# Sigmoid and one silu from tanh, and one logarithm for both image halves, in a four-layer convolution and Mamba kernel

## The chip, the cores and the metric

The kernel runs on one core of a Trainium2 chip, as one program. The metric is the device time of one execution in microseconds (us); the median of several executions is given. All data are float32.

## The reference

The input x has 8 images of 384 channels and 32 x 32 pixels. Four layers follow one another. The change lies in the first two, so only these are shown in detail.

```python
# layer 0
x_norm = x * rsqrt(mean_over_channels(x * x) + 1e-6) * norm_w
# mamba, run once forward and once over the flipped sequence of the 1024 pixels
u, z = split(x_flat @ in_proj_w.T)            # 384 channels each
u = silu(causal_conv1d(u) + conv1d_b)
dt, Bm, Cm = split(u @ x_proj_w.T)
delta = softplus(dt @ dt_proj_w.T + dt_proj_b)
h = exp(delta * A) * h + delta * u * Bm        # 16 states per channel, pixel after pixel
y = (sum_over_states(h * Cm) + u * D) * silu(z)
global_feat = (fwd + bwd) @ out_proj_w.T * scale_mod
local_feat = sigmoid(conv3x3_depthwise(x_norm) + dw_b) * x_norm
x = x + res_scale * (global_feat + local_feat)
# layer 1
h = conv1x1(bn2(conv3x3_depthwise(conv1x1(bn1(x))))); x1 = h + x
qp, kp = phi(q), phi(k)                        # phi(t) = exp(t - t*t/2), 8 heads of 48
zz = 1 / (qp . sum_over_pixels(kp) + 1e-6)     # one per head and pixel
x2 = x1 + proj((qp @ (kp^T v)) * zz)
xn = (x2 - mean) * rsqrt(var + 1e-5)           # over channels
x = x2 + gelu(xn @ mlp_w1 + b1) @ mlp_w2 + b2
# layers 2 and 3: large depthwise convolutions, a 1x1 convolution, an exact gelu
```

## The kernel before, in words

The 384 channels are three tiles of 128 partitions (NC = 3), and an image of 1024 pixels is two halves of 512 (HALF)[...]. Layers 0 and 1 are in one function, `_layers01`; layers 2 and 3 follow for all images at once and are not touched.

Three generators produce the work of one image.

`front(b)` (line 572) is layer 0 up to the scan. For each half it squares x on ACT (ScalarE), takes the mean over the channels and its inverse root in `rsqrt_mean`, and scales x on DVE (VectorE). Then it projects x to u and z (lines 596 to 604): the u half is copied out of PSUM, the z half goes through Silu, and both are stored in HBM from ACT's DMA queue. Then the 3 x 3 convolution of the local branch runs on PE (TensorE), ACT takes its Sigmoid (line 615), and DVE multiplies by x_norm and adds to x (lines 618 and 619). Last come the u convolution with its Silu (line 645) and the softplus, which is made of Abs, Relu, Exp and Ln (lines 671 to 678).

`scan(b)` (line 695) is the recurrence. It has 48 passes (2 directions, 2 halves, 3 channel tiles, 4 groups of 4 states), each of two units. A unit takes two Exps on ACT (tile `da`, line 776), one product on DVE (`du`, line 781), two scan instructions on DVE (`hs`, line 793), one product on POOL (GpSimd, line 802), and PE then sums over the states into `acc` (line 736). There are four `da` buffers and eight `hs` buffers.

`layer1(b)` (line 877) is the second layer of one image: out projection, 1 x 1 convolution, 3 x 3 convolution, 1 x 1 convolution, keys and values pixel block by pixel block (phi is a Square and an Exp, lines 874 and 875), queries, the denominator `den` (line 1010) with its reciprocal `rz` made as exp(-ln(den)) (lines 1014 and 1015), its spreading over the channels by a matmul (`rzb`, line 1021), the projection, the layer norm (lines 1034 to 1051, again with `rsqrt_mean`) and the MLP with its Gelu (line 1062).

The loop at the end of `_layers01` goes over the images. While image b is scanned, `front(b + 1)` and `layer1(b - 1)` are advanced between the passes of the scan, each in proportion to the cost that it yields. `defer(n, fn)` puts work off until n + 1 passes have gone by. Within what this order gives as priority, a scheduler places the instructions of each engine and hands out the buffers; each engine then runs its instructions strictly in order. Short-lived tiles come from one tag, `t2`, of eleven buffers of 128 x 512.

An ACT function belongs to a table that has to be loaded first. The instruction ACT_TABLE_LOAD is placed by the compiler wherever the next function is not in the loaded table.

Of the kernel before, what the change touches and what calls it, by code (L numbers as in the profile page):

```python
# [8 lines left out]
FP = mybir.dt.float32  # L9
AF = mybir.ActivationFunctionType  # L10
ALU = mybir.AluOpType
# [3 lines left out]
P = 128  # L15
C = 384
NC = C // P
# [3 lines left out]
HALF = 512  # L21
# [353 lines left out]
def _layers01(tc, nc, B, xv, x2_d, dram, ident, mean_w, eps5, eps6, one, half, minus1, vec, bns, bnt,  # L375
# [12 lines left out]
    with ExitStack() as ctx:  # L388
        wp = ctx.enter_context(tc.tile_pool(name="w0", bufs=1))
# [23 lines left out]
        x1v, zv, udv, yfv = chunks(x1_d), chunks(z_d), chunks(ud_d), chunks(yf_d)  # L413
# [5 lines left out]
        def const(ap, shape, tag):  # L419
            t = wp.tile(shape, FP, tag=tag, name=tag)  # L420
            nc.scalar.dma_start(t, ap)
            return t

        wx = const(xproj_t.rearrange("(k p) e -> p k e", p=P), [P, NC, 64], "wx")
        wdt = wp.tile([P, C], FP, tag="wdt", name="wdt")
# [3 lines left out]
        spread = wp.tile([P, 4, P], FP, tag="spread", name="spread")  # L429
# [2 lines left out]
            nc.gpsimd.memset(spread[32 * j : 32 * j + 1, j, :], 1.0)  # L432
        t1 = const(taps1, [P, 2 * NG, 32], "t1")
        selt = const(sel, [P, 32], "selt")
        neg_a = const(alog, [P, NG, NR], "neg_a")
        nc.scalar.activation(neg_a, neg_a, AF.Exp)
        nc.vector.tensor_scalar_mul(neg_a, neg_a, -1.0)
        mask = const(headmask, [PR, PR], "mask")
        m8 = const(mask8.rearrange("(k p) e -> p k e", p=P), [P, NC, 32], "m8")
        nc.scalar.dma_start(wdt[32:64, :], mask8_t)  # L440


        zero = wp.tile([P, C + NC + 1], FP, tag="zero", name="zero")
# [12 lines left out]
        def psum(name):  # L456
            return psp.tile([P, HALF], FP, tag="mm", name=name, bufs=2)

        def long_psum(name):
            return psp.tile([P, HALF], FP, tag="mo", name=name)  # L460

        def t2(name):
            return sp.tile([P, HALF], FP, tag="t2", name=name, bufs=N_T2)
# [19 lines left out]
        def defer(n, fn):  # L483
            e = [n, fn]
            late.append(e)
            return e
# [29 lines left out]
        def rows(t):  # L516
            return t.rearrange("p (h w) -> p h w", w=W)
# [29 lines left out]
            )  # L547
            return ps

        def rsqrt_mean(srcs, eps, name):  # L550

            stat = psum(f"{name}_s")
            for k, src in enumerate(srcs):
                for j in range(4):
                    nc.tensor.matmul(
                        stat[32 * j : 32 * j + 32, 0:P], mean_w[:, 0:32], src[:, j * P : (j + 1) * P],
                        start=(k == 0), stop=(k == NC - 1), skip_group_check=True,
                    )
            r = t2(f"{name}_r")[:, 0:P]
            nc.scalar.activation(r, stat[:, 0:P], AF.Ln, bias=eps)  # L560
            nc.scalar.activation(r, r, AF.Exp, scale=-0.5)
            ps = psum(f"{name}_b")
            for j in range(4):
                nc.tensor.matmul(
                    ps[:, j * P : (j + 1) * P], spread[:, j, :], r, start=True, stop=True,
                    skip_group_check=True,
                )
            return ps

        def front(b):

            xn = []
            for h in range(2):
                cols = bass.ts(h, HALF)
                xh = a6(f"xi_{b}_{h}")
                nc.sync.dma_start(xh, xv[b][:, :, cols])
                sqs = [t2(f"sq_{b}_{c}_{h}") for c in range(NC)]
                for c in range(NC):  # L580
                    nc.scalar.activation(sqs[c], xh[:, c, :], AF.Square)
                rstd = rsqrt_mean(sqs, eps6, f"ms_{b}_{h}")
                t, mid = image6(f"xn_{b}_{h}")
                for c in range(NC):
                    nc.vector.scalar_tensor_tensor(
                        mid[c], rows(xh[:, c, :]), vec("norm_w", c), rows(rstd), ALU.mult, ALU.mult
                    )
                put_image(xn_d, b % 2, h, t, nc.gpsimd)
                xn.append(mid)
                yield 3  # L590
            uo = u_d[b % 2].rearrange("(c p) i -> p c i", p=P)
            for e in range(2):
                w = wtile(inproj_t[:, e * C : (e + 1) * C], f"win_{b}_{e}")
                for h in range(2):
                    for m in range(NC):
                        ps = psum(f"in_{b}_{e}_{m}_{h}")
                        dense(ps, w, m, xn[h])
                        t = t2(f"uz_{b}_{e}_{h}_{m}")
                        if e == 0:
                            nc.scalar.copy(t, ps)  # L600
                            nc.scalar.dma_start(uo[:, m, 3 + h * HALF : 3 + (h + 1) * HALF], t)
                        else:
                            nc.scalar.activation(t, ps, AF.Silu)
                            nc.scalar.dma_start(zv[b][:, m, bass.ts(h, HALF)], t)
                        yield 3


# [1 line left out]
            for h in range(2):  # L609
                for c in range(NC):  # L610
                    xr = t2(f"xr_{b}_{h}_{c}")
                    nc.sync.dma_start(xr, xv[b][:, c, bass.ts(h, HALF)])
                    ps = conv3(xn_d, b % 2, h, c, t3, f"lc_{b}_{h}_{c}")
                    lc = t2(f"lg_{b}_{c}_{h}")
                    nc.scalar.activation(lc, ps, AF.Sigmoid, bias=vec("dw_b0", c))

                    def local(h=h, c=c, lc=lc, xr=xr):
                        nc.vector.tensor_mul(rows(lc), rows(lc), xn[h][c])
                        nc.vector.scalar_tensor_tensor(xr, lc, rs, xr, ALU.mult, ALU.add)
                        nc.gpsimd.dma_start(x1v[b][:, c, bass.ts(h, HALF)], xr)  # L620

                    defer(1, local)
                    yield 3


            for h in range(2):
                cols = bass.ts(h, HALF)
                ucs = [a6(f"uc_{b}_{h}_{d}") for d in range(2)]
                for c in range(NC):
                    uts = []  # L630
                    for j in range(4):
                        ut = sp.tile([P, 18 * (W + 2)], FP, tag="im", name=f"ut_{b}_{h}_{c}_{j}", bufs=N_IM)
                        src = bass.AP(
                            u_d.tensor, u_d[b % 2, 32 * (4 * c + j), h * HALF].offset,
                            [[UL, 32], [1, 4], [1, HALF + 3]],
                        )
                        nc.sync.dma_start(ut[:, 0 : HALF + 3], src)
                        uts.append(ut)
                    for d in range(2):
                        ps = psum(f"c1_{b}_{h}_{c}_{d}")  # L640
# [8 lines left out]
                ps = psum(f"xd_{b}_{h}")  # L649
                for k in range(NC):  # L650
                    for d in range(2):
                        nc.tensor.matmul(
                            ps[64 * d : 64 * d + 64, :], wx[:, k, :], ucs[d][:, k, :],
                            start=(k == 0), stop=(k == NC - 1), skip_group_check=True,
# [7 lines left out]
                for c in range(NC):  # L662
                    dls, ts = [], []
                    for d in range(2):
                        ps = psum(f"dt_{b}_{h}_{d}_{c}")
                        at = slice(64 * d, 64 * d + DTR)
# [3 lines left out]
                        t, dl = t2(f"sp_{b}_{h}_{d}_{c}"), t2(f"dl_{b}_{h}_{d}_{c}")  # L670
# [206 lines left out]
        def layer1(b):  # L877
# [34 lines left out]
            for h in range(2):  # L912
# [19 lines left out]
                skip_group_check=True,  # L932
# [62 lines left out]
            yield 4  # L995


            qps, rzs, xns = [], [], []
            for h in range(2):
                qp = a6(f"qp_{b}_{h}")  # L1000
                qps.append(qp)
                for m in range(NC):
# [1 line left out]
                    dense(ps, wq, m, xx[h])  # L1004
                    phi(qp[:, m, :], ps, f"q_{b}_{h}_{m}")
                    yield 3
            for h in range(2):
                den = long_psum(f"den_{b}_{h}")
                for k in range(NC):
                    nc.tensor.matmul(  # L1010
                        den[32:64, :], ksv[:, k, :], qps[h][:, k, :], start=(k == 0), stop=(k == NC - 1)
                    )
                rz = t2(f"rz_{b}_{h}")
                nc.scalar.activation(rz[32:64, :], den[32:64, :], AF.Ln, bias=eps6[32:64])
                nc.scalar.activation(rz[32:64, :], rz[32:64, :], AF.Exp, scale=-1.0)
                rzs.append(rz)
                yield 3
            for h in range(2):
                for k in range(NC):
                    ps = long_psum(f"rzb_{b}_{h}_{k}")  # L1020
                    nc.tensor.matmul(
                        ps, wdt[32:64, k * P : (k + 1) * P], rzs[h][32:64, :], start=True, stop=True
                    )
                    nc.vector.tensor_mul(qps[h][:, k, :], qps[h][:, k, :], ps)
                yield 3
            for h in range(2):
                for m in range(NC):
                    ps = long_psum(f"pj_{b}_{h}_{m}")
# [5 lines left out]
            for h in range(2):  # L1034
                mu = long_psum(f"mu_{b}_{h}")
                for k in range(NC):
                    nc.tensor.matmul(mu, mean_w, xx[h][:, k, :], start=(k == 0), stop=(k == NC - 1))
                xn = a6(f"ln_{b}_{h}")
                xns.append(xn)
                for k in range(NC):  # L1040
                    nc.vector.tensor_sub(xn[:, k, :], xx[h][:, k, :], mu)
                yield 3
            for h in range(2):
                xn = xns[h]
                sqs = [t2(f"vs_{b}_{h}_{k}") for k in range(NC)]
                for k in range(NC):
                    nc.scalar.activation(sqs[k], xn[:, k, :], AF.Square)
                rstd = rsqrt_mean(sqs, eps5, f"var_{b}_{h}")
                for k in range(NC):
                    nc.vector.tensor_mul(xn[:, k, :], xn[:, k, :], rstd)  # L1050
                yield 3

            for h in range(2):
                acc = [long_psum(f"mo_{b}_{h}_{m}") for m in range(NC)]
# [159 lines left out]
```

## Time and profile before

| | |
|---|---|
| time before, median of 3 | 5797.18 us (5793.76 to 5818.33) |
| span of the profiled run | 5805.1 us |
| PE busy | 4813.5 us, 83% |
| DVE busy | 3677.1 us, 63% |
| ACT busy | 3064.5 us, 53% |
| POOL busy | 2892.9 us, 50% |
| mean granted TensorE clock | 0.896 |

A row of an instruction group reads: line, engine, operation, tile written and tiles read, shapes, count, then busy us and the mean ns of one, then the idle time of the engine just before these instructions and what ended most of it. PE busy time is modelled, since matmuls overlap, so a PE that is 90% busy need not be at its peak. PE's weight loads (PEld) run beside its matmuls. A float32 matmul shows as two records.

### The profile page before, as it was taken

The page shows a single profiled execution, that of the slowest core. Times are in us where ns is not written, and L with a number is a line of the kernel's source. Part 1 is how long each engine was busy: PE and PEld are TensorE (multiplying, and loading weights), DVE is VectorE, ACT ScalarE, POOL GpSimd, SP SyncE. Part 2 cuts the span into 40 slices and gives each one's busy share as a digit, 9 for nine tenths or more (in the row PEclk, how much of TensorE's full clock was granted, in tenths as well). Part 3 has the DMA queues.
Part 4 walks back from the last instruction along what each step waited for, and adds up shares of the span by engine and source line. Part 5 has one row for each costly group of instructions (what it writes and reads, how often), then busy time and mean ns, then how long its engine had stood idle before and what let it go on. Part 6 is the DMA issues. An engine that isn't in the chain of part 4 may idle for free. (4 is left out here: it accounts for less than half of the span.)

```text
span 5805.1 us, 57844 instructions
## 1 busy us (share of the span) xinstructions
PE 4813.5 (83%) x19550; PEld 2091.8 (36%) x19550; DVE 3677.1 (63%) x3775; ACT 3064.5 (53%) x4116; POOL 2892.9 (50%) x1603
## 2 busy tenths in 40 slices
PE   4576579977988799879888997899779869899999
PEld 1121124322332243223322332233223324498498
DVE  0399997968687768776878786878678811011211
ACT  1656546874667557846784687468635613000211
POOL 3277676557554656565656564656466700110133
PEclk7687689988999899989999998899889989999999
DMA  9555476677567756764666467646643541366677
GB/s 299 185 176 178 145 247 194 230 188 216 187 197 202 216 173 193 168 204 134 191 205 189 141 175 186 190 140 176 179 145 120 135 96 45 95 165 158 196 166 150
DMA packets 528255, 1012.16 MB, mean 174 GB/s; under 512 B 60616, under 2 KB 196248, under 8 KB 527960
## 3 DMA queue, kind: packets, MB, share of 16 engines
q1 hardware_dynamic: 387952, 665.99, 38.5%
q0 software_dynamic: 71136, 248.53, 16.6%
q10 hardware_dynamic: 68872, 93.95, 5.1%
q8 instruction: 155, 2.54, 0.2%
q14 instruction: 140, 1.15, 0.1%
HBM read 763.86 MB, written 288.36 MB: 181 GB/s over the span
## 5 line engine op out<-in xcount | busy, mean ns | idle before, releaser
L802 POOL TENSOR_TENSOR hs<-hs,bct 128x1024 f32<-128x1024 f32 x768 | 2378.7, 3098 | 1180.4 <-DVE hs L793 665.8
L776 ACT ACTIVATE da<-dlt,neg_a 128x512 f32<-128x512 f32 x1536 | 1031.7, 714 | 848.8 <-DVE hs L793 756.8
L793 DVE TENSOR_TENSOR_SCAN hs<-da,carry,du 128x512 f32<-128x512 f32 x768 | 947.1, 1268 | 445.8 <-PE acc L736 211.0
L781 DVE TENSOR_TENSOR du<-vr,bct 128x1024 f32<-128x1024 f32 x768 | 1048.3, 1365 | 51.7 <-issue 21.7
L793 DVE TENSOR_TENSOR_SCAN hs<-da,du 128x512 f32<-128x512 f32 x768 | 901.2, 1208 | 153.9 <-ACT da L776 74.0
L736 PE MATMUL acc<-hs,selt 128*32 128x512 f32 x3072 | 736.5, 674 | 293.0 <-POOL hs L802 241.7
L1064 PE MATMUL mo<-hm,w 128*128 128x512 f32 x1152 | 562.5, 628 | 84.4 <-ACT hm L1062 60.8
L502 PE MATMUL mf<-ln,w 128*128 128x512 f32 x1152 | 545.7, 614 | 42.8 <-ACT dl L672 40.4
L736 PEld LDWEIGHTS acc<-hs,selt 128*32 128x32 f32 x3072 | 122.3, 115 | 722.2 <-POOL hs L802 391.6
L1064 PEld LDWEIGHTS mo<-hm,w 128*128 128x128 f32 x1152 | 214.9, 197 | 427.8 <-issue 255.1
L776 ACT ACT_TABLE_LOAD x265 | 340.0, 1283 | 39.2 <-DVE hs L793 26.7
L502 PEld LDWEIGHTS mf<-ln,w 128*128 128x128 f32 x1152 | 215.2, 194 | 358.9 <-issue 285.1
L316 PE MATMUL cv_b<-xt_b,toep 128*64 128x256 f32 x2688 | 304.5, 388 | 14.1 <-DVE xt_b L298 14.1
L316 PE MATMUL cv_a<-xt_a,toep 128*64 128x256 f32 x2688 | 304.6, 388 | 9.2 <-DVE xt_a L298 9.2
L502 PE MATMUL in<-xn,win 128*128 128x512 f32 x576 | 289.1, 633 | 26.0 <-ACT phi_k L874 24.2
L511 PE MATMUL dw<-dw_i,t3b 96*32 96x512 f32 x1152 | 238.0, 707 | 86.4 <-DMA dw_i<-h_d 86.3
L316 PEld LDWEIGHTS cv_b<-xt_b,toep 128*64 128x64 f32 x2688 | 282.5, 199 | 36.6 <-issue 16.2
L316 PEld LDWEIGHTS cv_a<-xt_a,toep 128*64 128x64 f32 x2688 | 282.4, 199 | 31.1 <-issue 10.4
L511 PE MATMUL lc<-lc_i,t 96*32 96x512 f32 x1152 | 218.1, 679 | 57.2 <-issue 28.8
L511 PE MATMUL c<-ut,t 128*32 128x512 f32 x768 | 195.2, 676 | 45.6 <-DMA ut<-u_d 32.1
L502 PE MATMUL op<-g,wo 128*128 128x512 f32 x288 | 143.1, 647 | 86.7 <-DMA g<-g_d 58.7
L1062 ACT ACTIVATE hm<-mf,biasf 128x512 f32<-128x512 f32 x192 | 130.7, 687 | 145.2 <-PE mf L502 143.5
(189 smaller groups left out, 5618.3 us busy)
## 6 DMA issues: line engine op xcount, KB each, us to landing
dlt<-dl_d SPq DMA_DIRECT2D x384, 256.0 KB, 4.5
vr<-v_d SPq DMA_DIRECT2D x384, 256.0 KB, 4.7
bct<-bc_d SPq DMA_DIRECT2D x256, 256.0 KB, 4.1
ut<-u_d SPq DMA_DIRECT2D x192, 257.5 KB, 5.0
lc_i<-xn_d SPq DMA_DIRECT2D x192, 228.8 KB, 4.9
dw_i<-h_d SPq DMA_DIRECT2D x192, 228.8 KB, 4.1
tp_d<-g_d POOLq DMA_DIRECT2D x64, 672.0 KB, 7.2
w<-w_d SPq DMA_DIRECT2D x64, 576.0 KB, 5.8
```

Source lines behind the costliest of these rows:

```text
L316: nc.tensor.matmul(ps[2 * H * e : 2 * H * (e + 1), 0:BW], tp[:, 2 * (g % (GB // 2)) + e, :, :, t].rearrange("p c j -> p (c j)"), rhs, star ...
L502: nc.tensor.matmul(ps, w[:, k, m * P : (m + 1) * P], rhs[k] if isinstance(rhs, list) else rhs[:, k, :], start=(k == 0), stop=(k == NC - 1),)
L511: nc.tensor.matmul(ps[32 * j : 32 * j + 32, :], lhs(j, i), rhs(j, i), start=(i == 0), stop=(i == taps - 1), skip_group_check=True,)
L736: nc.tensor.matmul(acc[32 * j : 32 * j + 32, :], selt, hs[j // 2][:, bass.ts(j % 2, HALF)], start=(r == 0), stop=(r == NR - 1), skip_group ...
L776: nc.scalar.activation(da[:, bass.ts(j, HALF)], dlt[:, bass.ts(j, HALF)], AF.Exp, scale=neg_a[:, g, r : r + 1],)
L781: nc.vector.tensor_mul(pairs(du), pairs(vt), bct[r][:, 0:1, :].to_broadcast([P, 2, HALF]),)
L793: nc.vector.tensor_tensor_scan(t[:, s][:, way], da[:, s][:, way], du[:, s][:, way], k_c if second else 0.0, ALU.mult, ALU.add,)
L802: nc.gpsimd.tensor_mul(pairs(t), pairs(t), bct[r][:, 1:2, :].to_broadcast([P, 2, HALF]))
L1062: nc.scalar.activation(hm, ps, AF.Gelu, bias=biasf[:, NC * i + f, :])
L1064: nc.tensor.matmul(acc[m], wb[:, f, m * P : (m + 1) * P], hm, start=(i == 0 and f == 0), stop=(i == FF // C - 1 and f == NC - 1),)
```

## The change

Four edits, all meant to have ACT change its table less often.

- The Sigmoid of the local branch becomes a Tanh: sigmoid(t) = (tanh(t/2) + 1) / 2. ACT computes tanh(t/2), with the halved bias `dwh`. DVE adds one and multiplies by x_norm in one scalar_tensor_tensor in place of the multiplication, and the factor 1/2 goes into `rsh`, half of the residual scale.
- The Silu of z becomes z/2 * (tanh(z/2) + 1). ACT writes the tanh into a new tile `th` and z/2 into `t`, both from PSUM. A new DVE instruction (`gate`) joins them two passes of the scan later, and the store of z goes from ACT's DMA queue to POOL's, behind that instruction.
- The reciprocal of the denominator is taken for both halves at once: `den` of half 0 is written to partitions 64 to 95 and of half 1 to 96 to 127 of one PSUM bank, so that one Ln and one Exp do for both. The matmuls of the two halves alternate, and the mask that spreads the result, `m8t`, lies on the same two groups of partitions.
- `rsqrt_mean` takes several halves: layer 1 squares both, puts both sets of sums into one bank, and takes one Ln and one Exp of 256 columns. In the front it still gets one half at a time.

```diff
-        def rsqrt_mean(srcs, eps, name):
+        def rsqrt_mean(halves, eps, name):
+            n = len(halves)
             stat = psum(f"{name}_s")
...
-            nc.scalar.activation(r, stat[:, 0:P], AF.Ln, bias=eps)
+            nc.scalar.activation(r, stat[:, 0 : n * P], AF.Ln, bias=eps)
             nc.scalar.activation(r, r, AF.Exp, scale=-0.5)
...
-                            nc.scalar.activation(t, ps, AF.Silu)
-                            nc.scalar.dma_start(zv[b][:, m, bass.ts(h, HALF)], t)
+                            th = t2(f"th_{b}_{h}_{m}")
+                            nc.scalar.activation(th, ps, AF.Tanh, scale=0.5)
+                            nc.scalar.activation(t, ps, AF.Copy, scale=0.5)
+                            def gate(h=h, m=m, t=t, th=th):
+                                nc.vector.scalar_tensor_tensor(t, th, one, t, ALU.add, ALU.mult)
+                                nc.gpsimd.dma_start(zv[b][:, m, bass.ts(h, HALF)], t)
+                            defer(1, gate)
...
-                    lc = t2(f"lg_{b}_{c}_{h}")
-                    nc.scalar.activation(lc, ps, AF.Sigmoid, bias=vec("dw_b0", c))
+                    lc = t2(f"lg_{b}_{c}_{h}")
+                    nc.scalar.activation(lc, ps, AF.Tanh, bias=dwh[:, c, :], scale=0.5)
...
-                        nc.vector.tensor_mul(rows(lc), rows(lc), xn[h][c])
-                        nc.vector.scalar_tensor_tensor(xr, lc, rs, xr, ALU.mult, ALU.add)
+                        nc.vector.scalar_tensor_tensor(
+                            rows(lc), rows(lc), one, xn[h][c], ALU.add, ALU.mult
+                        )
+                        nc.vector.scalar_tensor_tensor(xr, lc, rsh, xr, ALU.mult, ALU.add)
...
-            for h in range(2):
-                den = long_psum(f"den_{b}_{h}")
-                for k in range(NC):
+            den = long_psum(f"den_{b}")
+            for k in range(NC):
+                for h in range(2):
+                    at = slice(64 + 32 * h, 96 + 32 * h)
                     nc.tensor.matmul(
-                        den[32:64, :], ksv[:, k, :], qps[h][:, k, :], start=(k == 0), stop=(k == NC - 1)
+                        den[at, :], ksv[:, k, :], qps[h][:, k, :], start=(k == 0), stop=(k == NC - 1),
+                        skip_group_check=True,
                     )
-                rz = t2(f"rz_{b}_{h}")
-                nc.scalar.activation(rz[32:64, :], den[32:64, :], AF.Ln, bias=eps6[32:64])
-                nc.scalar.activation(rz[32:64, :], rz[32:64, :], AF.Exp, scale=-1.0)
...
+            rz = t2(f"rz_{b}")
+            nc.scalar.activation(rz[64:, :], den[64:, :], AF.Ln, bias=eps6[64:])
+            nc.scalar.activation(rz[64:, :], rz[64:, :], AF.Exp, scale=-1.0)
...
+            for k in range(NC):
+                for h in range(2):
+                    at = slice(64 + 32 * h, 96 + 32 * h)
                     ps = long_psum(f"rzb_{b}_{h}_{k}")
+                    nc.tensor.matmul(ps, m8t[at, bass.ts(k, P)], rz[at, :], start=True, stop=True)
                     nc.vector.tensor_mul(qps[h][:, k, :], qps[h][:, k, :], ps)
...
+            sqs = []
             for h in range(2):
+                sqs.append([t2(f"vs_{b}_{h}_{k}") for k in range(NC)])
+                for k in range(NC):
+                    nc.scalar.activation(sqs[h][k], xns[h][:, k, :], AF.Square)
+            yield 3
+            for h, rstd in enumerate(rsqrt_mean(sqs, eps5, f"var_{b}")):
                 xn = xns[h]
...
```

More of the change, by code (lines that the diff above doesn't have):

```diff
@@ L434, in _layers01 @@
         selt = const(sel, [P, 32], "selt")
+        dwh = wp.tile([P, NC, 1], FP, tag="dwh", name="dwh")
+        for c in range(NC):
+            nc.vector.tensor_scalar_mul(dwh[:, c, :], vec("dw_b0", c), 0.5)
+        rsh = wp.tile([P, 1], FP, tag="rsh", name="rsh")
+        nc.vector.tensor_scalar_mul(rsh, rs, 0.5)
         neg_a = const(alog, [P, NG, NR], "neg_a")
@@ L439, in _layers01 @@
         m8 = const(mask8.rearrange("(k p) e -> p k e", p=P), [P, NC, 32], "m8")
-        nc.scalar.dma_start(wdt[32:64, :], mask8_t)
+        m8t = wp.tile([P, C], FP, tag="m8t", name="m8t")
+        for h in range(2):
+            nc.scalar.dma_start(m8t[64 + 32 * h : 96 + 32 * h, :], mask8_t)
         zero = wp.tile([P, C + NC + 1], FP, tag="zero", name="zero")
@@ L548, in conv3 @@
             return ps
-        def rsqrt_mean(srcs, eps, name):
+        def rsqrt_mean(halves, eps, name):
+            n = len(halves)
             stat = psum(f"{name}_s")
-            for k, src in enumerate(srcs):
+            for i, srcs in enumerate(halves):
+                for k, src in enumerate(srcs):
+                    for j in range(4):
+                        nc.tensor.matmul(
+                            stat[32 * j : 32 * j + 32, bass.ts(i, P)], mean_w[:, 0:32], src[:, bass.ts(j, P)],
+                            start=(k == 0), stop=(k == NC - 1), skip_group_check=True,
+                        )
+            r = t2(f"{name}_r")[:, 0 : n * P]
+            nc.scalar.activation(r, stat[:, 0 : n * P], AF.Ln, bias=eps)
+            nc.scalar.activation(r, r, AF.Exp, scale=-0.5)
+            for i in range(n):
+                ps = psum(f"{name}_b{i}")
                 for j in range(4):
                     nc.tensor.matmul(
-                        stat[32 * j : 32 * j + 32, 0:P], mean_w[:, 0:32], src[:, j * P : (j + 1) * P],
-                        start=(k == 0), stop=(k == NC - 1), skip_group_check=True,
-                    )
-            r = t2(f"{name}_r")[:, 0:P]
-            nc.scalar.activation(r, stat[:, 0:P], AF.Ln, bias=eps)
[L561 to L568, printed above, removed]
+                        ps[:, bass.ts(j, P)], spread[:, j, :], r[:, bass.ts(i, P)], start=True, stop=True,
+                        skip_group_check=True,
+                    )
+                yield ps
         def front(b):
@@ L581, in front @@
                     nc.scalar.activation(sqs[c], xh[:, c, :], AF.Square)
-                rstd = rsqrt_mean(sqs, eps6, f"ms_{b}_{h}")
+                rstd, = rsqrt_mean([sqs], eps6, f"ms_{b}_{h}")
                 t, mid = image6(f"xn_{b}_{h}")
@@ L614, in front @@
                     lc = t2(f"lg_{b}_{c}_{h}")
-                    nc.scalar.activation(lc, ps, AF.Sigmoid, bias=vec("dw_b0", c))
+                    nc.scalar.activation(lc, ps, AF.Tanh, bias=dwh[:, c, :], scale=0.5)
                     def local(h=h, c=c, lc=lc, xr=xr):
-                        nc.vector.tensor_mul(rows(lc), rows(lc), xn[h][c])
-                        nc.vector.scalar_tensor_tensor(xr, lc, rs, xr, ALU.mult, ALU.add)
+                        nc.vector.scalar_tensor_tensor(
+                            rows(lc), rows(lc), one, xn[h][c], ALU.add, ALU.mult
+                        )
+                        nc.vector.scalar_tensor_tensor(xr, lc, rsh, xr, ALU.mult, ALU.add)
                         nc.gpsimd.dma_start(x1v[b][:, c, bass.ts(h, HALF)], xr)
@@ L995, in layer1 @@
             yield 4
-            qps, rzs, xns = [], [], []
+            qps, xns = [], []
             for h in range(2):
@@ L1006, in layer1 @@
                     yield 3
-            for h in range(2):
-                den = long_psum(f"den_{b}_{h}")
-                for k in range(NC):
+            den = long_psum(f"den_{b}")
+            for k in range(NC):
+                for h in range(2):
+                    at = slice(64 + 32 * h, 96 + 32 * h)
                     nc.tensor.matmul(
-                        den[32:64, :], ksv[:, k, :], qps[h][:, k, :], start=(k == 0), stop=(k == NC - 1)
-                    )
-                rz = t2(f"rz_{b}_{h}")
-                nc.scalar.activation(rz[32:64, :], den[32:64, :], AF.Ln, bias=eps6[32:64])
-                nc.scalar.activation(rz[32:64, :], rz[32:64, :], AF.Exp, scale=-1.0)
[L1016 to L1019, printed above, removed]
+                        den[at, :], ksv[:, k, :], qps[h][:, k, :], start=(k == 0), stop=(k == NC - 1),
+                        skip_group_check=True,
+                    )
+            rz = t2(f"rz_{b}")
[3 more added lines that the diff above has]
+            for k in range(NC):
+                for h in range(2):
+                    at = slice(64 + 32 * h, 96 + 32 * h)
                     ps = long_psum(f"rzb_{b}_{h}_{k}")
-                    nc.tensor.matmul(
-                        ps, wdt[32:64, k * P : (k + 1) * P], rzs[h][32:64, :], start=True, stop=True
-                    )
+                    nc.tensor.matmul(ps, m8t[at, bass.ts(k, P)], rz[at, :], start=True, stop=True)
                     nc.vector.tensor_mul(qps[h][:, k, :], qps[h][:, k, :], ps)
-                yield 3
+                yield 1
             for h in range(2):
@@ L1042, in layer1 @@
                 yield 3
+            sqs = []
             for h in range(2):
+                sqs.append([t2(f"vs_{b}_{h}_{k}") for k in range(NC)])
+                for k in range(NC):
+                    nc.scalar.activation(sqs[h][k], xns[h][:, k, :], AF.Square)
+            yield 3
+            for h, rstd in enumerate(rsqrt_mean(sqs, eps5, f"var_{b}")):
                 xn = xns[h]
[L1045 to L1048, printed above, removed]
                 for k in range(NC):
                     nc.vector.tensor_mul(xn[:, k, :], xn[:, k, :], rstd)
-                yield 3
+            yield 3
             for h in range(2):
```

## The prediction

> **What bounds the kernel now.** First the busy time of each engine by stretch, to see which part the change lies in. Columns: length, then busy us of PE, PE weight loads, DVE, ACT, POOL, the granted TensorE clock, DMA share, GB/s. The stretches are the first image's front, the eight scans, the last image's layer 1 alone, and layers 2 and 3.
>
> ```profile
> 0.00:215.00 215.00, 113.30 (x372) 33.30 (x372) 27.09 (x76) 60.55 (x84) 56.63 (x111) 0.75 0.86 272
> 215.00:4647.00 4432.00, 3648.08 (x12584) 1301.66 (x12585) 3485.79 (x3453) 2830.86 (x3734) 2657.30 (x1279) 0.89 0.61 180
> 4647.00:5010.00 363.00, 309.10 (x905) 131.25 (x904) 31.57 (x46) 71.68 (x106) 11.05 (x20) 0.91 0.28 69
> 5010.00:5805.00 795.00, 742.99 (x5693) 625.59 (x5691) 132.66 (x201) 101.44 (x193) 167.89 (x193) 0.97 0.66 164
> ```
>
> The change touches the first three rows. The scans take 4432 us, about 550 us an image, and no engine fills them: PE 82%, DVE 79%, ACT 64%, POOL 60%. So the bound must change inside an image. The same table for one image (2000 to 2495 us), cut where its work changes:
>
> ```profile
> 2000.00:2060.00 60.00, 53.15 (x208) 17.56 (x206) 48.31 (x43) 25.72 (x41) 40.98 (x18) 0.86 0.85 267
> 2060.00:2170.00 110.00, 106.46 (x377) 48.09 (x376) 68.43 (x63) 72.99 (x104) 56.21 (x26) 0.95 0.47 151
> 2170.00:2260.00 90.00, 81.74 (x362) 29.57 (x361) 86.82 (x99) 64.89 (x80) 57.24 (x24) 0.96 0.52 161
> 2260.00:2450.00 190.00, 173.41 (x516) 56.81 (x516) 134.21 (x123) 158.19 (x188) 108.61 (x56) 0.96 0.69 193
> ```
>
> Row two (keys and values, queries, and the z half of the input projection) is PE's: 106 of 110 us. Row three (layer norm, local convolution) is DVE's: 87 of 90. Row four (the MLP beside the u convolution and softplus) is nearest ACT's: 158 of 190. The waits say the same. Engine and line, what it waited for, total us, times, longest: the first two over the whole run, the third from 2260 to 2450 alone.
>
> ```profile
> DVE hs L793 <- PE acc L736: 255.4, 54, 21.9
> DVE hs L793 <- ACT da L776: 254.0, 82, 16.4
> ...
> DVE hs L793 <- ACT da L776: 35.1, 14, 4.6
> ```
>
> The scan on DVE loses as much to PE as to ACT, and its loss to ACT falls in the MLP stretch: 35.1 us in one image, against 254.0 in all.
>
> Third, ACT's groups by line, for what it spends on tables.
>
> ```profile
> L776 ACT ACT_TABLE_LOAD x265 | 340.0, 1283 | 39.2 <-DVE hs L793 26.7 <-DMA dlt<-dl_d 4.3 <-issue 3.6
> L1062 ACT ACT_TABLE_LOAD x150 | 192.4, 1283 | 3.6 <-ACT da L776 1.0
> ...
> L603 ACT ACT_TABLE_LOAD x43 | 55.2, 1283 | 15.2 <-PE in L502 14.2 <-ACT uz L600 0.4
> L615 ACT ACT_TABLE_LOAD x43 | 55.2, 1283 | 1.5 <-ACT uz L603 0.4 <-ACT yt L746 0.4
> ```
>
> All such rows add up to 776 loads, 996 us of ACT's 3064. The largest row is the way back: da is an Exp, and whatever was put between two da pays one load to leave Exp and one to return.
>
> **What the Trainium skill says.** "ScalarE: Activation LUTs", section "What ACT_TABLE_LOAD costs": a switch is 1283 ns plus a drain of about 1380 ns, 2.66 us in all. The trace agrees with the 1283 but shows no drain: the idle ahead of 265 loads is 39.2 us, 0.15 us each. I price a load at 1.283. Section "Table sets: the hidden batching unit" of that page puts tanh into the set of exp, sigmoid into another, and Ln and Exp into a common one. The program order of the changed kernel has tanh beside da without a load. For Ln and Exp the trace before disagrees: 22 loads stand ahead of the Exp of line 561, so each pair is two sets here. "TensorEngine Tiling (Array Packing)", "Key Properties": tiles on other rows or columns of the array run in parallel. The trace agrees: 3072 records acc<-hs,selt of mean 674 ns are 2070 us end to end and only 736.5 us busy. "DMA: Bandwidth & Descriptors", "Issuing engines are not separate DMA queues": moving a transfer saves only the issue time; the z stores give back 0.33 us of ACT's sequencer each and should cost 0.58 us of POOL, as the x1 stores of line 620 do.
>
> **The change part by part.**
>
> 1. *Table loads.* The built program of the changed kernel has 593 loads for 776: 183 fewer, 235 us of ACT. About 86 are the loads of z and of the local gate, 64 are returns (da 265 to 220, keys' Exp 19 to 0), 16 belong to rz, and 20 to the two logarithms of the means. The Gelu loads (150 to 148) and those of the u silu stay.
> 2. *z.* A silu at 597 ns becomes a tanh, taken at the same, and a scaled copy, which the trace does not show in this form; bounds are 577 ns (the copy of line 600) and 613 (the price of the skill's page for 512 elements with immediates). I take 0.6: 48 x 0.6 = 29 us more on ACT, in the PE-bound stretch, where ACT has 37 us of 110 to spare. The bank of PSUM is let go 1.2 us after the first of the two begins, not 1.9 (load and silu).
> 3. *The gate of z on DVE.* 48 scalar_tensor_tensor, at 0.74 us when undisturbed (line 890) and 0.82 as line 619 has it among POOL's work: 36 to 39 us. They fall into the PE-bound stretch, where DVE is busy 68 of 110, so hidden. The gate can wait for its tanh and copy, and behind it on DVE stand the next du and scan, for which POOL and PE wait; behind the z store on POOL stands the multiply hs. The two passes of deferral and the placing of each gate a few da behind its copy make that wait short.
> 4. *The local gate.* tensor_tensor (1490 ns mean, undisturbed 0.67) becomes scalar_tensor_tensor (0.74 to 0.82): from +0.1 to -0.67 us each, 48 times, +5 to -32 us of DVE. As line 619 directly follows it and may inherit the disturbance, I take -10, in the DVE-bound stretch.
> 5. *rz and the variance.* Eight Ln and Exp pairs of 1.3 us and eight of 0.68 go, for longer ones at about +0.2: -14 us of ACT. More telling is who waits: PE waited 34.1 us, 13 times, for the Exp of line 561 ahead of var_b; a chain of two loads per half becomes one per image, so I take half, 17 us in all, against which the first half now stands behind the squares of the second, 3 x 0.62 us, 8 images: 15 us at most, mostly hidden by other matmuls.
> 6. *den and rzb.* Same number of matmuls, but h 0 and h 1 now alternate on different columns (den) and rows (rzb). Busy now 43.7 and 57.7 us; halved at best: -51 us of PE, 6 an image, in the PE-bound stretch. I take 5.
>
> By stretch, for each of the six scans with both front and layer 1: PE-bound 5 (part 6); DVE-bound 1 to 2 (part 4); MLP stretch: about three of the six local gates fall in it, 3 x 2 loads x 1.283 = 7.7, and 2 of the variance's waits, less what PE takes over (it is busy 173 of 190): 6. Together 12 to 13, six times: 75. The seventh scan has layer 1 but no front: 5 to 6. The last layer 1 alone loses 6 loads (11 to 5 after the last da), 7.7 us, of which PE waited 5.5 for var_b, and 5 of packing: 10. Sum 91; I keep five sixths, since some of it will be given back at the image's end, where PE is busy 16 us from 2450 to 2495 while it waits for loads of g. That is 76: 5797 - 76 = 5721.
>
> **The rivals.**
>
> *Hidden.* Most removed loads stand where ACT is waiting anyhow: it waits 756.8 us for the scan, and the z loads lie in PE's stretch. Then only part 6 in half and the last image count: about 25 us, 5772, or nothing, 5797. Against it stand 254 us of DVE waiting for da, part of it behind loads that go.
>
> *Slower.* The gate and its store put two more in-order links between ACT, DVE and POOL. For it: th and the held z take two of the eleven t2 buffers each for two passes, the six squares of both halves take six at once, and in the trace ACT already waited 33.3 us for dl stores ahead of the squares of line 581, which is how a shortage of these buffers looks. If each of 48 gates stops DVE for 1 us, costs its 0.74 and its store holds POOL for 0.58, that is 111 us, less half of the gain: 5797 + 111 - 38 = 5870; milder, 5825. Against: that stretch has DVE 42 and POOL 54 us free of 110.
>
> *Larger.* ACT's order, not its load, paces PE and DVE everywhere: 235 - 29 + 14 = 220 us off ACT, three quarters of it on the path: 5632.
>
> **How the numbers follow.** Forecast case (gain of 30 to 135 us) 0.57, hidden 0.18, slower 0.15, larger 0.10. Faster by over 0.5% (below 5768) takes the first and last, 0.67, and a little of hidden: 0.68; within, 0.17; slower, 0.15. The range runs from the edge of the larger case, 5635, to the mild form of the slower one, 5820; 0.1 is left out on either side.
>
> **What would show it.** Right: ACT's busy time down by about 220 us, to 2845; no loads at z, and nearly none at the local gate; DVE's wait for da below 254, by 40 or more; den and rzb at half their busy time; DVE busy the same within 40 us; the scans together near 4365 us. Wrong: ACT's wait for the scan up by what its loads lost and the span the same (hidden); or DVE waiting tens of us for the copy of z, POOL for the gate, or ACT for z stores to free buffers (slower).

## The result, and the profile after

The changed kernel takes 5882.32 us (5870.15 to 5893.75), beside 5802.22 us (5793.76 to 5818.33) for the kernel before: 1.0134 of it, 95% interval 1.0101 to 1.0167. It is 80 us slower where 76 us of gain were forecast. The mean granted TensorE clock of the profiled execution is 0.890 for 0.896, but PE's busy time is 15 us less (4798.6 for 4813.5), so slower matmuls do not account for the 80 us.

The stretches first, cut where the same work begins and ends as in the table of before (front, scans, last layer 1, layers 2 and 3; columns as there).

```profile
0.00:215.00 215.00, 118.10 (x372) 33.77 (x372) 31.46 (x85) 58.16 (x85) 58.44 (x112) 0.74 0.86 267
215.00:4742.00 4527.00, 3637.76 (x12602) 1297.09 (x12604) 3547.41 (x3500) 2607.30 (x3575) 2665.73 (x1331) 0.88 0.60 177
4742.00:5096.00 354.00, 303.06 (x896) 129.83 (x892) 30.39 (x45) 64.52 (x98) 8.69 (x19) 0.93 0.27 69
5096.00:5886.00 790.00, 739.67 (x5682) 624.39 (x5682) 131.39 (x199) 100.65 (x192) 164.54 (x192) 0.97 0.67 165
```

The whole loss is in the scans, 4432 to 4527 us, with 224 us less work on ACT. The last layer 1, which has no scan beside it, is 9 us shorter. The same passes of one image (2000 to 2450 us before, in four rows of 60, 110, 90 and 190):

```profile
2040.00:2088.00 48.00, 39.76 (x182) 12.43 (x181) 45.38 (x39) 20.21 (x32) 36.19 (x13) 0.93 0.86 258
2088.00:2202.00 114.00, 105.08 (x380) 48.11 (x379) 76.17 (x64) 59.33 (x99) 58.57 (x34) 0.97 0.50 159
2202.00:2312.00 110.00, 96.03 (x388) 34.12 (x386) 92.19 (x106) 52.51 (x68) 56.41 (x25) 0.95 0.48 152
2312.00:2510.00 198.00, 166.23 (x509) 54.39 (x508) 133.14 (x129) 161.62 (x193) 111.45 (x61) 0.92 0.69 176
```

The four rows together take 470 us for 450. The cuts do not split the work in quite the same way (the third row holds 388 records of PE for 362), so single rows compare less exactly than their sum. ACT does 52.5 us of work in the third row, for 64.9, and the row is 20 us longer. In the fourth, the MLP stretch in which the gain was expected, ACT is as busy as before (161.6 for 158.2), DVE waits 39.9 us for `da`, for 35.1, and the row is 8 us longer. No engine fills a larger share of these two rows than before: what was added is in the main time in which the engines wait for one another. The waits over the whole run (engine and line, what it waited for, total us, times, longest):

```profile
ACT da L796 <- DVE hs L813: 1018.7, 399, 19.8
...
DVE hs L813 <- ACT da L796: 271.6, 79, 15.3
...
DVE hs L813 <- PE acc L756: 235.3, 54, 21.1
...
POOL z_d L620 <- DVE uz L619: 115.4, 28, 11.9
...
DVE uz L619 <- ACT uz L616: 65.6, 14, 18.2
```

ACT's wait for the scan rose by 262 us (756.8 before), more than the 234 that its busy time fell (3064.5 to 2830.6). DVE waits no less for `da` (254.0 before). The last two lines are new: the gate of z waits for ACT's copy (38.3 of the 65.6 us in the scans, the rest in the first front), and its store on POOL waits for the gate. The table loads and the edited groups of DVE and PE:

```profile
L796 ACT ACT_TABLE_LOAD x220 | 282.3, 1283 | 39.6 <-issue 14.4 <-DMA dlt<-dl_d 12.4 <-DVE hs L813 8.7
L1084 ACT ACT_TABLE_LOAD x148 | 189.9, 1283 | 6.5 <-ACT da L796 2.9 <-DMA v_d<-sp 0.9
...
L633 ACT ACT_TABLE_LOAD x2 | 2.6, 1283 | 0.0
```

```profile
L639 DVE SCALAR_TENSOR_TENSOR xr<-lg,rsh,xr 128x512 f32<-128x512 f32 x48 | 52.7, 1097 | 0.6
L636 DVE SCALAR_TENSOR_TENSOR lg<-lg,one,xn 128x512 f32<-128x512 f32 x48 | 48.4, 1007 | 117.9 <-ACT lg L633 102.9 <-DMA x_d<-xr 15.0
L619 DVE SCALAR_TENSOR_TENSOR uz<-th,one,uz 128x512 f32<-128x512 f32 x48 | 43.4, 905 | 65.6 <-ACT uz L616 65.6
```

```profile
L1043 PE MATMUL rzb<-rz,m8t 32*128 32x512 f32 x96 | 50.6, 898 | 22.6 <-DVE qp L1044 13.5 <-ACT rz L1037 9.1
L1031 PE MATMUL den<-qp,ks 128*32 128x512 f32 x96 | 23.4, 597 | 0.9 <-ACT qp L895 0.9
```

So the loads went as counted, and `den` is halved; `rzb` is not (57.7 before).

### The profile page after: what moved, and what is told of

Same layout as the page of the kernel before. It is cut to its first block, busy times and chain, and to the rows that moved or that the text cites. A ratio compares the mean times of both kernels' runs of the same rounds, so it can differ in the third digit from the quotient of the medians.

```text
span 5886.7 us, 57671 instructions
## 1 busy us (share of the span) xinstructions
PE 4798.6 (82%) x19550; PEld 2085.1 (35%) x19550; DVE 3740.6 (64%) x3827; ACT 2830.6 (48%) x3949; POOL 2897.4 (49%) x1651
## 5 line engine op out<-in xcount | busy, mean ns | idle before, releaser
L801 DVE TENSOR_TENSOR du<-vr,bct 128x1024 f32<-128x1024 f32 x768 | 1065.0, 1387 | 48.3 <-DMA vr<-v_d 20.0
L518 PE MATMUL c<-ut,t 128*32 128x512 f32 x768 | 205.9, 695 | 65.6 <-DMA ut<-u_d 53.8
L298 DVE COPY xt_b<-xt_b 64x2480 f32<-64x2480 f32 x24 | 38.7, 1612 | 262.6 <-DMA xt_b<-xp_d 262.6
```

What stands on the lines that cost most here:

```text
L298: nc.vector.tensor_copy(half1[:, :, 0 : XL - 1], half0[:, :, 1:XL])
L518: nc.tensor.matmul(ps[32 * j : 32 * j + 32, :], lhs(j, i), rhs(j, i), start=(i == 0), stop=(i == taps - 1), skip_group_check=True,)
L801: nc.vector.tensor_mul(pairs(du), pairs(vt), bct[r][:, 0:1, :].to_broadcast([P, 2, HALF]),)
```

## The experiments

All ratios are to the kernel before, run beside it on the same chip, with the 95% interval in brackets. Four parts were tried first, each alone in the kernel before, under three theories: *links* (the gate of z and its store put engines in a row), *place* (merged logarithms push the MLP and the softplus together at an image's end), *DVE time* (the added DVE instructions are what costs).

**1. The local gate alone** (tanh, and the scalar_tensor_tensor that adds one).

```diff
-nc.scalar.activation(lc, ps, AF.Sigmoid, bias=vec("dw_b0", c))
+nc.scalar.activation(lc, ps, AF.Tanh, bias=dwh[:, c, :], scale=0.5)
-nc.vector.tensor_mul(rows(lc), rows(lc), xn[h][c])
+nc.vector.scalar_tensor_tensor(rows(lc), rows(lc), one, xn[h][c], ALU.add, ALU.mult)
```

> The kernel before with the local gate alone made from tanh (line 615 to 619). Theory of the links (the gate of z with its store costs the time): no z gate here, so 15 to 40 us faster than before, since some 86 table loads with their returns are fewer and DVE gets no instruction more. Theory of the place (the merged logarithms push the MLP and softplus together at the image's end): also faster or the same. Theory of DVE time (each instruction made slower on DVE is paid for): within 10 us of before.

5849.99 us, 1.0097 [1.0080, 1.0114], with 89 loads fewer. None of the three theories forecast a loss of this size.

**2. The z part alone** (tanh, copy, gate on DVE, store from POOL).

```diff
-nc.scalar.activation(t, ps, AF.Silu)
+nc.scalar.activation(th, ps, AF.Tanh, scale=0.5)
+nc.scalar.activation(t, ps, AF.Copy, scale=0.5)
+defer(1, gate)
```

> The kernel before with the silu of z alone made from tanh, with the gate on DVE and the store from POOL. Theory of the links: slower than before by 50 us or more, 5850 to 5890. Theory of the place: within 20 us of before. Theory of DVE time: 48 instructions of about 0.9 us, 43 us slower.

5878.43 us, 1.0154 [1.0140, 1.0168]: the dearest part alone, as *links* forecast.

**3. The merged denominators alone.**

```diff
-den = long_psum(f"den_{b}_{h}")
...
-yield 3    # after den, for each of two h
...
-yield 3    # after rzb, for each of two h
+den = long_psum(f"den_{b}")
...
+yield 3    # after den, once
...
+yield 1    # after rzb, for each of three k
```

> The kernel before with one logarithm for the denominators of both halves, with its den and rzb matmuls alternating. Theory of the links: 10 to 40 us faster, from matmuls that overlap and 16 loads fewer. Theory of the place: slower by 20 us or more, because the six units of cost that go from the generator of layer 1 move what comes after it.

5850.35 us, 1.0100 [1.0086, 1.0114], as *place* forecast.

**4. The merged logarithms of the variance alone.**

```diff
-rstd = rsqrt_mean(sqs, eps5, f"var_{b}_{h}")
+for h, rstd in enumerate(rsqrt_mean(sqs, eps5, f"var_{b}")):
```

> The kernel before with one logarithm for the variances of both halves. Theory of the links: within 20 us of before. Theory of the place: slower by 30 us or more, as the MLP of the first half has to wait for the squares of the second and Gelu, the u silu and softplus then fall together.

5744.52 us, 0.9925 [0.9911, 0.9938]: faster by 47 us. *Place* as stated falls, and *links* had it within 20 us. That number 3, with 7 loads fewer and `den` at half its busy time, loses 59 us pointed at what it changes besides: the cost that it yields to the loop falls from 12 to 6, so that everything after it is handed out earlier. Two theories for the next four: *placing* and *own cost*, told in the expectations.

**5 and 6. Only the pace.** The work of layer 1 and of the next front is handed out 3% later, and 3% earlier.

```diff
-while work and done < need * (i + 1) / (rounds - 1):
+while work and done < 0.97 * need * (i + 1) / (rounds - 1):   # 6: 1.03
```

> The kernel before with the work of layer 1 and of the next front handed out 3% later against the scan (factor 0.97 on the threshold of the loop over the passes); no operation is added or removed. In the built order the mean Gelu step of the MLP stands at pass 41.5 of the scan for 40.3. Theory 'placing' (the time follows where that work falls against the scan: later is faster, earlier slower, as with the merged variance logarithms, at 41.3 and 47 us faster, and the merged denominators, at 39.2 and 59 us slower): 5720 to 5770. Theory 'own cost' (each edit's time is that of the operations and waits it adds): no change, 5775 to 5805.

5797.56 us, 1.0058 [1.0045, 1.0070].

> The same with factor 1.03, the work handed out 3% earlier; mean Gelu step at pass 39.9 for 40.3. Placing: slower, 5805 to 5840. Own cost: no change, 5775 to 5805.

5812.49 us, 1.0083 [1.0070, 1.0096]. Both are slower, so "later is faster" falls, and so does *own cost*, which forecast no change. What stands: these moves, which change no operation, cost 0.6 and 0.8%, nearly the size of what was lost in 1 and 3.

**7. The merged denominators with the yields kept.**

```diff
+yield 6    # after den, for 3
+yield 2    # for each k of rzb, for 1
```

> The merged denominators alone, as in the run that was 59 us slower than before, but with the costs that they yield to the loop put back to what the unmerged ones yield (6 and 3 x 2 in place of 3 and 3 x 1). The matmuls, logarithms and waits are those of the merged form; the mean Gelu step is back at pass 40.3. Placing: the loss is gone, 5765 to 5800. Own cost (the halves wait for one another, one long chain in place of two): 5835 to 5865.

5757.96 us, 0.9982 [0.9971, 0.9994]. Two numbers in yields are the whole difference to 1.0100. The traces show two places where DVE lost time: its wait for `acc` over the whole run, 290.0 us with the short yields and 215.6 with the kept ones, and its wait at the local gate in the scans, here first with the short yields and then with the kept ones:

```profile
DVE lg L620 <- ACT lg L617: 60.0, 9, 14.7
```

```profile
DVE lg L620 <- ACT lg L617: 9.5, 2, 7.7
```

**8. The whole change with the yields kept.**

> The whole change with those yields put back in the same way; mean Gelu step at pass 40.4 for 39.6. Placing: it regains most of the 59 us that the merged denominators lost alone, 5815 to 5850. Own cost: as the change, 5865 to 5895.

5805.10 us, 1.0069 [1.0055, 1.0083], for 1.0134: half of the change's loss was in the yields.

**9 and 10. The halves of the local gate.** ACT's tanh with DVE's multiplication kept; DVE's scalar_tensor_tensor with the sigmoid kept.

```diff
+nc.scalar.activation(lc, ps, AF.Tanh, bias=dwh[:, c, :], scale=0.5)                          # 9
+nc.vector.scalar_tensor_tensor(rows(lc), rows(lc), one, xn[h][c], ALU.add, ALU.mult)         # 10
```

> The ACT half of the local gate's edit alone: tanh of half the value in place of the sigmoid, 83 table loads fewer in the built program, DVE's tensor_tensor kept. The output is not the reference's, since the + 1 and the half of x are left out. Ratios to the kernel before. Theory 'displaced' (an edit of this size moves the scheduler's order, and any move from the order of before costs 0.6 to 1%, as moving the work 3% either way did): 1.005 to 1.012, near the 1.0097 of the whole edit. Theory 'DVE' (the loss of the local gate lies in its scalar_tensor_tensor): 0.99 to 1.002.

5808.75 us, 1.0070 [1.0056, 1.0084]. This run takes 83 loads away and adds nothing, and is slower. The waits of the local gate in the scans, before and here:

```profile
ACT lg L615 <- PE lc L511: 6.2, 7, 2.5
...
DVE lg L618 <- ACT lg L615: 3.6, 3, 1.5
```

```profile
ACT lg L620 <- PE lc L516: 40.6, 13, 7.5
...
DVE lg L623 <- ACT lg L620: 33.8, 9, 11.8
```

Over the whole run, ACT's busy time fell by 113 us, to 2951.0, and this line grew by 152 from 756.8:

```profile
ACT da L781 <- DVE hs L798: 908.6, 391, 12.8
```

ACT gives all of it back: to the scan, and to the convolution. That PE has not finished the convolution because ACT comes without a load ahead of it is argued; with the loads put back (17), ACT still waits 38.6 us there in the scans, for 58.5 in the same kernel without them (12) and 12.0 with the sigmoid (11).

The order moved too. By the order in which instructions start in the two traces (by tile names, table loads left out), at least 191 of ACT's 3340 instructions and 290 of DVE's 3775 stand at another place than before.

> The DVE half alone: the sigmoid and its loads kept, the tensor_tensor of the local gate replaced by the scalar_tensor_tensor of the change. The output is not the reference's, since a sigmoid stands where a tanh is expected. Theory 'DVE': it carries the whole loss, 1.008 to 1.015. Theory 'displaced': also slower, but by what its own order costs, 1.003 to 1.010; the two halves together then come to more than the whole edit's 1.0097.

5743.96 us, 0.9959 [0.9947, 0.9972]: faster, so the loss isn't in DVE's instruction. *Displaced* misses as well: here too the order moved (at least 152 of ACT's instructions, 284 of DVE's), and the kernel gained 0.4%. Not every move costs. Numbers 1 and 9, both with the tanh, have nearly the same order (6 and 9 instructions apart) and differ by 0.3%.

**11 and 12. The parts that gained, together; then with the local gate.** Denominators (yields kept) and variance; the same with the local gate of the change, z left a silu.

> Merged denominators with the yields kept, and merged variance logarithms; neither tanh. If what the parts gave alone adds up (0.9982 and 0.9925): 0.988 to 0.994. If each order has its own cost, as 'displaced' says, the sum isn't to be relied on: anywhere from 0.985 to 1.003, and its scans need not be shorter by the sum.

5719.24 us, 0.9913 [0.9901, 0.9926]; the parts add up.

> The whole change with the yields kept and z left a silu (local gate, denominators, variance). If the parts add up: 0.998 to 1.003. If the loss of the local gate alone was one of its order: 0.985 to 0.996. The change with the yields kept was 1.0069, so this also says what the z part costs in its company: 0.7 to 0.9% by the sum of the parts alone.

5779.75 us, 1.0022 [1.0014, 1.0030]: they add up here too, and the local gate costs 1.1% in this company, for 1.0% alone. The z part does not add up: between this kernel and the change with the yields kept (1.0069) it costs 0.5%, where it cost 1.5% alone and 0.7 to 0.9% was forecast.

**13, 14 and 16. The gates a pass later.** The stalls of number 9 suggested that DVE comes too soon. The local gate's edit with its DVE part put off by three passes in place of two; the whole change with the yields kept and both gates put off in the same way; and the kernel before with its own gate put off, as the control. (The expectations count the passes one lower.)

```diff
-defer(1, local)
+defer(2, local)
```

> The whole edit of the local gate alone (1.0097 of before), with its DVE part put off by two passes of the scan and not one. Theory 'stall': without its load the tanh asks for the convolution sooner than PE has it, so ACT (33.8 to 48.6 us of DVE's wait for it in the slower runs, 3.6 to 9.5 in those that were no slower) and DVE stand still in order, with the exponentials and the scan behind them. One pass more takes DVE's wait away: below 10 us, and the ratio falls to 0.995 to 1.003. Theory 'displaced' (any move of the order costs): 1.004 to 1.012 as before.

5806.63 us, 1.0088 [1.0074, 1.0103]; DVE still waits 29.2 us for lg in the scans.

> The whole change with the yields kept (1.0069), with the local gate and the gate of z both put off by two passes. Stall: DVE's waits for lg and uz, 30.6 and 34.8 us there, fall below 10 each, and the ratio to 0.993 to 1.001. Displaced: 1.004 to 1.012.

5796.98 us, 1.0069 [1.0055, 1.0083]; the waits for lg and uz are 41.6 and 34.9 us.

> Control: the kernel before with its local gate put off by two passes, nothing else. DVE waits 3.6 us for lg there, so by 'stall' there is nothing to gain: 0.996 to 1.004. By 'displaced' it is slower, 1.004 to 1.010. A gain of over 0.5% would say that the later gate helps whatever the function is.

5791.88 us, 1.0068 [1.0054, 1.0082]. None was faster for it: the stalls are still there, so the theory that one pass more takes them away is wrong, and whether the edited kernels would be faster without them was not tried. The control is a third pure move that costs 0.7%, with at least 60 of ACT's instructions and 112 of DVE's at another place. In it DVE waits 5.9 us at the local gate in the scans, and 4.1 in number 6: a loss of this size needs no stall there.

**15. The faster parts and the two scalar_tensor_tensor, with the sigmoid.**

```diff
-nc.vector.tensor_mul(rows(lc), rows(lc), xn[h][c])
-nc.vector.scalar_tensor_tensor(xr, lc, rs, xr, ALU.mult, ALU.add)
+nc.vector.scalar_tensor_tensor(rows(lc), rows(lc), rs, xn[h][c], ALU.mult, ALU.mult)
+nc.vector.scalar_tensor_tensor(xr, lc, one, xr, ALU.mult, ALU.add)
```

> Merged denominators with the yields kept, merged variance logarithms (0.9913 together), and the DVE half of the local gate with the sigmoid kept: lg * rs * x_norm and then + x, both as scalar_tensor_tensor. The DVE half alone was 0.9959 with another form of the same instructions. If what the parts gave adds up: 0.985 to 0.990. Displaced: 0.990 to 1.000.

5670.73 us beside 5756.20: 0.9852 [0.9839, 0.9865], the fastest of all. Its scans:

```profile
215.00:4521.00 4306.00, 3573.42 (x12585) 1286.45 (x12586) 3467.63 (x3452) 2753.05 (x3660) 2662.18 (x1279) 0.90 0.61 185
```

The same work on every engine as before but for ACT's 78 us, PE's 75 and DVE's 18, in 126 us less. But the instruction is not the reason. The local gate in number 11, and here:

```profile
L623 DVE TENSOR_TENSOR lg<-lg,xn 128x512 f32<-128x512 f32 x48 | 72.0, 1501 | 131.3 <-ACT lg L620 131.3
```

```profile
L623 DVE SCALAR_TENSOR_TENSOR lg<-lg,rs,xn 128x512 f32<-128x512 f32 x48 | 75.4, 1571 | 129.2 <-ACT lg L620 129.2
```

It takes 3.4 us longer in all, while the kernel is 0.6% faster; DVE waits less for `acc`, 210.0 us for 252.0. What else the form of the instruction altered is the order that the scheduler made: at least 179 of ACT's 3308 instructions and 280 of DVE's 3775 stand at another place than in number 11.

**17. The loads put back with the tanh kept.** Number 12, with a sigmoid of one column ahead of each tanh.

```diff
+nc.scalar.activation(lc[:, 0:1], ps[:, 0:1], AF.Sigmoid)
 nc.scalar.activation(lc, ps, AF.Tanh, bias=dwh[:, c, :], scale=0.5)
```

> The change with the yields kept and z left a silu (1.0022), with a sigmoid of one column put ahead of each tanh of the local gate and overwritten by it: the tanh and all other work stay, the table loads come back (757 in the built program for 656), and so does the order that the scheduler gives to a gate with loads. The twin with a sigmoid and no tanh was 0.9852. If it is the missing loads, by way of the order and of ACT's arriving early at the convolution, that cost the 1.7%: 0.983 to 0.994. If it is the tanh or its DVE form: 1.000 to 1.006, the 48 small sigmoids adding some 10 us.

5785.56 us, 1.0042 [1.0029, 1.0055]. With 101 loads more than in number 12 it is 0.2% slower, and not 1.7% faster: the number of loads is not what separates the tanh from its twin with a sigmoid (15, with 727). The expectation puts this result down to the tanh or its DVE form, but its premise that the order comes back as well does not hold: at least 186 of the 3308 ACT instructions that the two have in common, and 286 of DVE's, stand at another place than in the twin.

```profile
DVE hs L806 <- ACT da L789: 311.9, 93, 18.9
DVE hs L806 <- PE acc L749: 172.8, 31, 20.6
```

Here DVE waits 87 us more for `da` than in the twin (225.0) and 37 us less for `acc` (210.0), with the same amount of work on DVE and 44 us more on ACT.

**18. The loads of z taken away, nothing put in.**

```diff
-nc.scalar.activation(t, ps, AF.Silu)
+nc.scalar.activation(t, ps, AF.Tanh, scale=0.5)
```

> The kernel before with the silu of z replaced by a tanh alone, no copy, no gate, the store as before: only the loads go (691 in the built program for 776). The output is not the reference's, since the tanh is stored in place of z/2 times (tanh + 1). The whole z part was 1.0154. If loads that stand in a PE-bound stretch are worth nothing and only their order costs, as at the local gate: 1.000 to 1.012. If these loads are worth time and the gate, the copy and the store carry the loss: 0.985 to 0.997.

5790.56 us, 1.0046 [1.0032, 1.0060]. 85 loads fewer and again no gain; ACT's wait for the scan is 848.1 us. At least 225 of ACT's instructions and 252 of DVE's moved. The rest of the z part (copy, gate, store) makes 1.0154 of 1.0046.

## Why the prediction was wrong

The change can be put together from the runs, one step at a time, each a ratio to before. A step holds the edit and the order that came with it; the runs do not separate the two.

| kernel | ratio | what the step adds |
|---|---|---|
| variance, denominators with yields kept (11) | 0.9913 | -0.9% |
| and the local gate (12) | 1.0022 | +1.1% |
| and z (8) | 1.0069 | +0.5% |
| and the short yields: the change | 1.0134 | +0.65% |

By the steps of the prediction:

1. *Table loads.* Right in number and in size: 593 in the built program, ACT busy 2830.6 us for 2845.
2. *z on ACT.* Right: tanh 587 ns and copy 588, between the two bounds, 28.2 us for the copies.
3. *The gate of z, "hidden" in the PE-bound stretch.* Its time is 43.4 us for 36 to 39. That it is hidden is wrong: tanh alone was 1.0046, with copy, gate and store 1.0154, though in the company of the other parts z as a whole cost only 0.5%. DVE waited 65.6 us at the gate, and POOL 115.4 for it. How copy, gate and store share the 1.1% was not separated. DVE's busy time rose by 63.5 us, more than the 40 allowed.
4. *The local gate on DVE, -10 us.* The two instructions together took 111.1 us and take 101.1. Right as a sum, and no use: the kernel's time doesn't follow it (15).
5. *rz and the variance.* PE's wait ahead of var_b went from 34.1 to 9.5 us in the change, as argued. The merged variance alone gave 0.75%, 47 us, more than was taken for both logarithms, but not by this wait: there it fell to 19.7 us, while PE's wait for the squares ahead of var_s rose from 4.6 to 19.9. Its order moved as well, so where its 47 us come from is open.
6. *den and rzb, 5 us an image.* den halved, rzb fell from 57.7 to 50.6, which the sum took as half. With the yields kept it is worth 0.18%, about 10 us or 1.3 an image. The same edit's yields, which the prediction did not price at all, cost 1.2% alone and 0.65% in the change.

The step that failed is the sum **by stretch**: "MLP stretch: about three of the six local gates fall in it, 3 x 2 loads x 1.283 = 7.7", and with it "Together 12 to 13, six times: 75". It failed in two ways.

First, these loads do not lie in that stretch. In each of the six images three of the local gates do come after the first Gelu, but all six are through before the fifth of 24. In the rows of before, one load of the gate stands in the second row and five in the third:

```profile
L615 ACT ACT_TABLE_LOAD x1 | 1.3, 1283 | 0.0
```

```profile
L615 ACT ACT_TABLE_LOAD x5 | 6.4, 1283 | 0.1
```

The fourth row has none. It holds 58 table loads before and 59 in the change, of the same kinds, so the change took no load from it. The loads that went lay in the rows that the prediction itself calls PE's and DVE's: 17 became 2 in the second row, 24 became 14 in the third. Without this term the same sum would give some 45 us of gain (6.5 six times, 5.5 and 10, five sixths of it), so the misplaced loads are only a part of the miss.

Second, the sum turned removed loads into time on the assumption that the order of all other work stays. Two runs removed loads and put no work in their place, at the local gate and at z, and got slower by 0.7% and 0.5%; in both, the order of the rest moved with them. The term that the sum lacks altogether, the yields, is 0.65% of the change's 1.34%.

As far as the load itself goes, the rival *hidden* was right, and its sign was there: ACT's wait for the scan up by what the loads lost. The other half of that sign, a span the same as before, did not come. The rival *slower* named the gate and its store, which are a part of the loss, but not the yields nor the local gate. The shortage of t2 buffers that it feared hardly shows: ACT waited 77 us for stores before and 90 in the change, none of it for a store of z. That its figure, 5870, lies near the measured 5882 is in good part luck: it priced the z gate at 111 us, and in the company of the other parts z cost 0.5%, about 27 us. The last layer 1, with no scan beside it, did as forecast: 9 us shorter for 10.

What stays open is why the orders with a tanh at the local gate are the bad ones: +0.7% in the kernel before, +1.4% between numbers 10 and 1, +1.7% between 15 and 12. Three pure moves of the order, which cost 0.6 to 0.8% each, and the two yields, at 1.2%, show that an order alone can do about this much, and number 10 that an order can gain as well. That it is the order here is argued and not shown, since no run kept the order and changed ACT's function.

## What to carry to other kernels

When a scheduler or a pacing loop sets the order, a changed instruction is also a changed order; measure first what a move alone costs (here 0.6 to 0.8%), and don't expect to read a smaller gain off the instruction. Before a removed instruction is credited to a stretch, list the instructions of that stretch and see that it is there. If an edit merges steps that yield a cost to a pacing loop, keep the sum of the yields, or the edit moves everything behind it. An engine that waits 757 us for another may give 235 us less work back as longer waits, as ACT did here; count a removed load as time only where it is shown ahead of something that others wait for.

## What was not expected of the hardware

The kernel before had medians of 5756 to 5802 us in different sets of runs, 0.8%, as much as most of the parts; times of different sets can't be compared as they stand. No kernel but that of before was timed in two sets, so how well a ratio carries from one set to another, as between 3 and 7 or between the change and 8, is not known.

What the local gate's multiplication costs on DVE goes more with where it lands than with its form. The scalar_tensor_tensor took 1571 ns in number 15, where the tensor_tensor took 1501 in 11, but 1007 in the change, where the tensor_tensor took 1490 before. Of the 48 instances before, the 17 with no POOL instruction beside them took at most 693 ns; all 24 that took over 1000 had one.
